# Two LSTMs inside a decoder: the inputs' share of the gates and the attention's values, in pieces of 128 columns, one in each step

## The chip, the cores and the metric

The kernel runs on one core of one Trainium2 chip. The metric is the device time of one execution in microseconds. Three runs of the kernel before gave 2397.09, 2397.65 and 2398.21 us; the median is 2397.65.

## What is computed

A decoder of four blocks, each with an attention, a cross attention and a feed-forward part, works on x of 8 sequences with 112 tokens and 256 features. The change lies in the first part alone, an attention whose queries and keys come from two LSTMs, and in which the two differ only by their weights:

```
xW = jnp.einsum('bsd,gd->sbg', x, Wih) + b
def step(carry, xt):
    h, c = carry
    gates = xt + h @ Whh.T
    i, f, g, o = jnp.split(gates, 4, axis=-1)
    c = jax.nn.sigmoid(f) * c + jax.nn.sigmoid(i) * jnp.tanh(g)
    h = jax.nn.sigmoid(o) * jnp.tanh(c)
    return ((h, c), h)
...
v = (hidden_states @ Wv.T + bv)
hq = _lstm(hidden_states, Wih_q, Whh_q, b_q)
hk = _lstm(hidden_states, Wih_k, Whh_k, b_k)
```

Small networks then turn hq and hk into queries and keys, and v is attended. Each LSTM has 112 steps that follow one on another: a step needs h of the step before it. The term xW needs no h, nor does v.

## The kernel before

All is in fp32. A step of one LSTM (line 645 on) is a chain over three engines. Eight matmuls on TensorE (line 649) multiply h with the 256 x 1024 recurrent weights. The batch is only 8, so h stands as weights of 128 x 32 and the gates' 1024 columns are moved past it in four quarters, each into its own 32 partitions of the PSUM tile g. ScalarE takes sigmoid and tanh of g (660, 661); VectorE makes the new cell in three operations (666, 668, 669); ScalarE its tanh (671); VectorE h (673) and its transpose hT (675), which is what the next step's matmuls wait for. GpSimd copies hT into hs, where the attention will find it (676). The two LSTMs, l = 0 and 1, take turns in each step t, so one's TensorE work lies beside the other's chain.

The inputs' share enters through TensorE as well. xw holds xW with its bias for 16 steps at a time (128 rows: 8 sequences x 16 steps). Four matmuls with a picking matrix as weights (`from_inputs`, line 627) start the tile g of step t + 1 with the right rows of xw, just after the recurrent matmuls of step t. xw itself is made by `inputs(m, l, half)` (line 617): two matmuls of 128 x 128 weights by 512 columns through the helper at line 410, then one addition of the bias on VectorE (622). The first four pieces, for steps 0 to 15, stand ahead of the loop; the other 24 are put at every fourth step (t = 2, 6, 10 and so on, lines 677 and 678). The PSUM tiles "mm" of these pieces have two buffers, and so has g.

After the loop, `l0_attn` makes the values: for each of the 8 sequences two matmuls of 112-column weights by 256 columns (line 569) and a bias addition (571). Then `l0_attend` begins with `unit` (line 705), whose matmuls take hs of the first LSTM, then of the second, and goes on to queries, keys, scores and the rest.

The order of each engine's instructions is settled when the program is built: a scheduler places them by priorities and estimated times, except inside a `tc.manual_schedule` block, where the engines named keep the order in which the code is written. Before the change the LSTMs are not in such a block. Weights lie in a ring of eight buffers, loaded through SyncE's queue when `w.done` frees buffers; the values' weights and bias are in the ring from the start.

In the trace each fp32 matmul instruction stands as two MATMULs, called passes below: a piece of 512 columns is four passes, line 649 is 16 per step and LSTM, line 627 is 8.

Of the kernel before, what the change touches and what calls it, by code (L numbers as in the profile page):

```python
# [24 lines left out]
AF = mybir.ActivationFunctionType  # L25
ALU = mybir.AluOpType
AX = mybir.AxisListType
ET = mybir.EngineType
PSUM = bass.MemoryType.PSUM

P = 128
S, NB, D = 112, 8, 256
# [323 lines left out]
class _Kernel:  # L356
# [198 lines left out]
    def l0_attn(self):  # L555
        nc, tc, w = self.nc, self.tc, self.w
        with ExitStack() as outer:
            keep = outer.enter_context(tc.tile_pool(name="l0a", bufs=1))
            hs = self.t(keep, [P, 2, 2, NB, S], "hs")
            vv = self.t(keep, [P, NB, 4, 64], "vv")  # L560
            with tc.tile_pool(name="ps_l0a", bufs=2, space=PSUM) as ps, tc.tile_pool(name="l0a_x", bufs=1) as px:
                xs = self.t(px, [P, 2, S // 16, NB, 16], "xs")
                self.ln_T_mm(ps, xs)
                self.lstm(hs, xs, ps)
                w.done("l0a_b_k")
                wv = w("l0a_wv", 2)
                bv = w("l0a_bv").rearrange("p (h d) -> p h d", h=4)
                for b in range(NB):
                    pm = self.t(ps, [P, 512], "mm")[:S, :D]
                    self.mm(pm, [(x, wv[:, k, :]) for k, x in enumerate(self.tokens(b))])  # L570
                    nc.vector.tensor_tensor(
                        vv[:S, b], pm.rearrange("p (h d) -> p h d", h=4), bv[:S], ALU.add
                    )
            self.l0_attend(hs, vv)
        w.done("l0a_bv")

# [16 lines left out]
                )  # L593
                self.nc.scalar.copy(self.xnT[:, kc, half * HT : (half + 1) * HT], tp[:, :HT])

    def lstm(self, hs, xs, ps0):

        nc, tc = self.nc, self.tc
        G = range(4)
        whh = [self.w("l0a_hh_q", 2), self.w("l0a_hh_k", 2)]
        wih = [self.w("l0a_ih_q", 2), self.w("l0a_ih_k", 2)]
        bias = [self.w("l0a_b_q"), self.w("l0a_b_k")]
        pick = self.c("pick").rearrange("p (r m) -> p r m", r=16)
        with tc.tile_pool(name="ps_lstm", bufs=2, space=PSUM) as ps, tc.tile_pool(  # L610
            name="lstm", bufs=2
        ) as work, tc.tile_pool(name="lstm_c", bufs=1) as cpool:

            xw = self.t(cpool, [P, 2, S // 16, 1024], "xw")
            cell = [self.t(cpool, [P, 64], f"cell{l}") for l in range(2)]

            def inputs(m, l, half):
                cols = slice(512 * half, 512 * half + 512)
                pm = self.t(ps0, [P, 512], "mm")
                steps = [xs[:, k, m, :, :].rearrange("p b r -> p (b r)") for k in range(2)]  # L620
                self.mm(pm, [(x, wih[l][:, k, cols]) for k, x in enumerate(steps)])
                nc.vector.tensor_tensor(xw[:, l, m, cols], pm, bias[l][:, cols], ALU.add)

            def from_inputs(t, l):
                g = self.t(ps, [P, 256], f"g{l}")
                for j in G:
                    nc.tensor.matmul(  # L627
                        g[32 * j : 32 * j + 32, :],
                        pick[:, t % 16, :],
                        xw[:, l, t // 16, 256 * j : 256 * j + 256],  # L630
                        start=True,
                        stop=t == 0,
                        skip_group_check=True,
                    )
                return g

            for l in range(2):
                for half in range(2):
                    inputs(0, l, half)
            later = [(m, l, half) for m in range(1, S // 16) for l in range(2) for half in range(2)]  # L640
            gs = [from_inputs(0, l) for l in range(2)]
            hT = [None, None]
            for t in range(S):
                for l in range(2):
                    g = gs[l]
                    if t > 0:
                        for c in range(2):
                            for j in G:
                                nc.tensor.matmul(  # L649
                                    g[32 * j : 32 * j + 32, :],  # L650
                                    hT[l][:, c, :],
                                    whh[l][:, c, 256 * j : 256 * j + 256],
                                    start=False,
                                    stop=c == 1,
                                    skip_group_check=True,
                                )
                    if t + 1 < S:
                        gs[l] = from_inputs(t + 1, l)
                    sg = self.t(work, [P, 256], f"sg{l}")
                    nc.scalar.activation(sg[:, :192], g[:, :192], AF.Sigmoid)  # L660
                    nc.scalar.activation(sg[:, 192:], g[:, 192:], AF.Tanh)
                    ig, fg, og, gg = (sg[:, 64 * i : 64 * i + 64] for i in range(4))
                    if t == 0:
                        nc.vector.tensor_tensor(cell[l], ig, gg, ALU.mult)
                    else:
                        nc.vector.tensor_tensor(cell[l], cell[l], fg, ALU.mult)
                        tmp = self.t(work, [P, 64], f"tmp{l}")
                        nc.vector.tensor_tensor(tmp, ig, gg, ALU.mult)
                        nc.vector.tensor_tensor(cell[l], cell[l], tmp, ALU.add)  # L669
                    th = self.t(work, [P, 64], f"th{l}")  # L670
                    nc.scalar.activation(th, cell[l], AF.Tanh)  # L671
                    h = self.t(work, [P, 64], f"h{l}")
                    nc.vector.tensor_tensor(h, og, th, ALU.mult)  # L673
                    hT[l] = self.t(work, [P, 2, 32], f"hT{l}")
                    nc.vector.transpose(hT[l].rearrange("p c b -> p (c b)"), h)  # L675
                    nc.gpsimd.tensor_copy(hs[:, l, :, :, t], hT[l][:, :, :NB])
                if t % 4 == 2 and later:
                    inputs(*later.pop(0))

    def l0_attend(self, hs, vv):  # L680

# [1563 lines left out]
```

## Time and profile before

| what | us |
|---|---|
| median of three runs | 2397.65 |
| profiled execution | 2397.02 |
| its span, first to last instruction | 2395.2 |
| first recurrent matmul (step 1) starts | 34.88 |
| recurrent matmuls of the last step start (first, second LSTM) | 428.50, 430.24 |
| values' matmuls | 429.50 to 437.8 |
| first matmul of the attention's first unit | 437.82 |

From 36 to 376 us, where the late pieces are, TensorE is counted busy 318 us, VectorE 204, ScalarE 131, GpSimd 43; the granted TensorE clock is 1.00. The bias additions are 28 of 0.692 us at line 622 and 8 of 0.424 us at line 571. The waits of that stretch are led, GpSimd's aside, by ScalarE's tanh for the cell (122.2 us over 183 times), weight loads of line 649 for hT (101.8 us), ScalarE's sigmoid for the recurrent matmuls (78.3 us) and h for the tanh (69.9 us).

How to read it: times are microseconds from the span's start. PE is TensorE's matmuls and PEld its weight loads, DVE is VectorE, ACT ScalarE, POOL GpSimd. `out<-in` are tiles by the program's names. A matmul's row gives its weights' shape (128*32) and its moving operand's (128x256); the start is recorded, the end is modelled, so that rows which follow one another overlap. A timeline merges equal instructions that follow each other into one row with a count; brackets give idle time of the engine before it and what ended that.

### The profile page before, as it was taken

Reading aid. Unit: us, or ns where it says so; the run is one execution under the profiler, and the core shown is the slowest. Engines: PE = TensorE matmul, PEld = TensorE weight load, DVE = VectorE, ACT = ScalarE, POOL = GpSimd, SP = SyncE. Lnnn points to the kernel's source line nnn. Section 1 sums busy time; section 2 is a strip of 40 time slices with the busy share of each in tenths; the row PEclk is TensorE's granted clock in tenths of the full one; section 3 lists DMA queues with packets and bytes.
Section 4 is the critical chain, followed back from the end, with each engine's and each line's share of the span. In section 5 each row is a group of like instructions: output and inputs, shape, how many; then the busy total and the mean of one; then the engine's idle time right before and its main releaser. Section 6 shows DMA issues by size and latency. Waiting matters only on the chain.

```text
span 2395.2 us, 43373 instructions
## 1 busy us (share of the span) xinstructions
PE 2135.7 (89%) x17096; PEld 1269.8 (53%) x17096; DVE 1427.7 (60%) x3994; ACT 774.4 (32%) x2157; POOL 216.3 (9%) x415
## 2 busy tenths in 40 slices
PE   6999999999898899899998869899999999899944
PEld 3444444466566566546664436466555556556622
DVE  4655566586455577543987557767740223667687
ACT  2333334462111355420111111466311110346522
POOL 0111111000011100000222331100000000200000
PEclk9999999899999999899999979999999999899956
DMA  4000000000100000001001011000111100000000
GB/s 188 2 2 2 2 20 35 30 19 18 53 1 15 19 2 19 18 27 53 1 19 36 19 44 38 16 2 19 53 36 63 42 0 1 1 1 2 2 0 16
DMA packets 10732, 55.95 MB, mean 23 GB/s; under 512 B 1834, under 2 KB 3626, under 8 KB 5793
## 3 DMA queue, kind: packets, MB, share of 16 engines
q1 hardware_dynamic: 8304, 44.57, 5.2%
q0 software_dynamic: 2080, 7.07, 0.9%
q8 instruction: 136, 2.23, 0.4%
q10 hardware_dynamic: 144, 1.54, 0.2%
q14 instruction: 68, 0.55, 0.1%
HBM read 52.23 MB, written 0.92 MB: 22 GB/s over the span
## 4 chain that ended last, share of the span: by engine, by line
PE 68%; DVE 20%; issue 5%; ACT 4%; DMA 2%; POOL 1%; DVEq 0%; ACTq 0%; POOLq 0%
PE mm L410 30%; PE gu L410 6%; PE tr L1197 6%; PE g L649 6%; PE sc L410 4%; PE av L1213 3%; PE tr L410 2%; DVE rot L1506 1%; ACT sg L660 1%; PE mm L799 1%; PE av L410 1%; ACT th L671 1%; DVE hT L675 1%; PE s L410 1%; DVE h L673 1%
## 5 line engine op out<-in xcount | busy, mean ns | idle before, releaser
L649 PE MATMUL g<-w,hT 128*32 128x256 f32 x3552 | 237.3, 384 | 26.2 <-DVE hT L675 25.9
L1197 PEld LDWEIGHTS tr<-cst,xe 112*125 112x125 f32 x1152 | 151.6, 188 | 94.7 <-issue 38.3
L1184 DVE TENSOR_REDUCE xnm<-sc 112x1 f32<-112x375 f32 x384 | 184.7, 541 | 28.6 <-PE sc L410 28.0
L410 PE MATMUL mm<-xnT,w 128*128 128x448 f32 x432 | 182.6, 560 | 18.8 <-DVE qT L1509 5.3
L1197 PE MATMUL tr<-cst,xe 112*125 112x112 f32 x1152 | 192.9, 289 | 7.1 <-DVE xeT L1205 4.3
L410 PE MATMUL mm<-hT,w 128*128 128x448 f32 x512 | 193.0, 539 | 0.0
L649 PEld LDWEIGHTS g<-w,hT 128*32 128x32 f32 x3552 | 95.4, 109 | 168.2 <-DVE hT L675 125.0
L410 PEld LDWEIGHTS mm<-hT,w 128*128 128x128 f32 x512 | 97.1, 190 | 94.4 <-issue 94.4
L627 PE MATMUL g<-xw,cst 128*32 128x256 f32 x1792 | 138.0, 379 | 0.0
L1205 DVE COPY xeT<-tr 125x336 f32<-125x336 f32 x192 | 97.3, 507 | 67.3 <-PE tr L1197 60.4
L1203 ACT COPY xeT<-tr 125x336 f32<-125x336 f32 x192 | 85.3, 444 | 159.4 <-PE tr L1197 159.4
L410 PEld LDWEIGHTS mm<-xnT,w 128*128 128x128 f32 x432 | 78.0, 193 | 104.2 <-issue 54.2
L410 PE MATMUL mm<-w,hT 128*112 128x256 f32 x576 | 131.8, 389 | 0.0
L1188 ACT ACTIVATE xe<-sc,xnm 112x375 f32<-112x375 f32 x256 | 126.6, 582 | 11.2 <-DVE xnm L1184 11.2
L410 PE MATMUL gu<-xnT,w 128*128 128x448 f32 x320 | 127.6, 554 | 1.6 <-DVE hT L1351 1.2
L410 PEld LDWEIGHTS mm<-w,hT 128*112 128x112 f32 x576 | 103.8, 182 | 26.8 <-issue 3.9
L660 ACT ACTIVATE sg<-g 128x192 f32<-128x192 f32 x224 | 74.1, 331 | 104.4 <-PE g L649 92.5
L671 ACT ACTIVATE th<-cell 128x64 f32<-128x64 f32 x224 | 57.4, 256 | 147.7 <-DVE cell L669 147.4
L673 DVE TENSOR_TENSOR h<-sg,th 128x64 f32<-128x64 f32 x224 | 50.5, 225 | 85.5 <-ACT th L671 85.5
L2099 DVE COPY wq<-tr 128x256 bf16<-128x256 bf16 (+1 forms) x12 | 4.6, 421 | 161.6 <-PE tr L2098 161.6
L410 PE MATMUL mm<-w,oT 128*112 128x256 f32 x288 | 75.8, 413 | 22.1 <-DVE oT L1686 13.8
L410 PEld LDWEIGHTS gu<-xnT,w 128*128 128x128 f32 x320 | 60.3, 193 | 61.5 <-issue 54.9
(404 smaller groups left out, 3667.9 us busy)
## 6 DMA issues: line engine op xcount, KB each, us to landing
w<-in_w SPq DMA_DIRECT2D x33, 1024.0 KB, 4.9
raw<-in_wq POOLq DMA_DIRECT2D x3, 1024.0 KB, 5.2
w<-in_w SPq DMA_DIRECT2D x3, 896.0 KB, 6.9
wi<-in_wint POOLq DMA_DIRECT2D x3, 768.0 KB, 6.2
w<-in_w SPq DMA_DIRECT2D x2, 768.0 KB, 4.4
ctxT<-in_ctxT ACTq DMA_DIRECT2D x1, 1500.0 KB, 8.3
cx<-in_ctx POOLq DMA_DIRECT2D x1, 1500.0 KB, 20.9
w<-in_w SPq DMA_DIRECT2D x2, 512.0 KB, 3.5
```

What stands on the lines that cost most here:

```text
L410: self.nc.tensor.matmul(out, lhsT, rhs, start=i == 0, stop=i == len(pairs) - 1)
L627: nc.tensor.matmul(g[32 * j : 32 * j + 32, :], pick[:, t % 16, :], xw[:, l, t // 16, 256 * j : 256 * j + 256], start=True, stop=t == 0, sk ...
L649: nc.tensor.matmul(g[32 * j : 32 * j + 32, :], hT[l][:, c, :], whh[l][:, c, 256 * j : 256 * j + 256], start=False, stop=c == 1, skip_group ...
L660: nc.scalar.activation(sg[:, :192], g[:, :192], AF.Sigmoid)
L671: nc.scalar.activation(th, cell[l], AF.Tanh)
L673: nc.vector.tensor_tensor(h, og, th, ALU.mult)
L1184: nc.vector.tensor_reduce(nm, sc, AX.X, ALU.max, negate=True)
L1188: nc.scalar.activation(e, sc, AF.Exp, bias=nm)
L1197: nc.tensor.transpose(tp[:CH, i * S : (i + 1) * S], e[:, i * CH : (i + 1) * CH], self.ident[:S, :S])
L1203: nc.scalar.copy(eT, src)
L1205: nc.vector.tensor_copy(eT, src)
L1213: nc.tensor.matmul(avs[b][32 * j : 32 * j + 32, c * S : (c + 1) * S], values[b % 2][:CH, i, 4 * c + j, :], eTs[b, c, j][:, i, :], start=i ...
```

## The change

`inputs` now takes a first column and a width. Ahead of the loop it still makes the four pieces of 512 columns; all else is cut into pieces of 128 columns: 6 x 2 x 8 = 96 of the inputs' share and, by a new function `values`, 8 x 2 = 16 of the values. They form one list of 112 in the order of need. One is made ahead of the loop and one in each step 0 to 110. Its matmuls are written after the second LSTM's matmuls and the picking matmuls for its next step; its bias addition is returned as a function and written on VectorE between the second LSTM's cell and its h. The loop is wrapped in a manual schedule of TensorE, VectorE and ScalarE. The loop over the values behind the LSTMs is gone, and the call that frees the LSTMs' weights stands behind both.

```
-                self.lstm(hs, xs, ps)
-                w.done("l0a_b_k")
-                wv = w("l0a_wv", 2)
...
-                for b in range(NB):
-                    pm = self.t(ps, [P, 512], "mm")[:S, :D]
-                    self.mm(pm, [(x, wv[:, k, :]) for k, x in enumerate(self.tokens(b))])
...
+                self.lstm(hs, xs, vv, ps)
+            w.done("l0a_b_k")
...
-            def inputs(m, l, half):
-                cols = slice(512 * half, 512 * half + 512)
-                pm = self.t(ps0, [P, 512], "mm")
+            def inputs(m, l, a, n):
+                cols = slice(a, a + n)
+                pm = self.t(ps0, [P, 512], "mm")[:, :n]
                 steps = [xs[:, k, m, :, :].rearrange("p b r -> p (b r)") for k in range(2)]
                 self.mm(pm, [(x, wih[l][:, k, cols]) for k, x in enumerate(steps)])
-                nc.vector.tensor_tensor(xw[:, l, m, cols], pm, bias[l][:, cols], ALU.add)
+                def biased():
+                    nc.vector.tensor_tensor(xw[:, l, m, cols], pm, bias[l][:, cols], ALU.add)
+                return biased
+            def values(b, half):
+                cols = slice(half * P, half * P + P)
+                pm = self.t(ps0, [P, 512], "mm")[:S, :P]
+                self.mm(pm, [(x, wv[:, k, cols]) for k, x in enumerate(self.tokens(b))])
+                out = vv[:S, b].rearrange("p h d -> p (h d)")[:, cols]
+                def biased():
+                    nc.vector.tensor_tensor(out, pm, bv[:S, cols], ALU.add)
+                return biased
...
-            later = [(m, l, half) for m in range(1, S // 16) for l in range(2) for half in range(2)]
+            pieces = [(inputs, m, l, P * i, P) for m in range(1, S // 16) for l in range(2) for i in range(8)]
+            pieces += [(values, b, half) for b in range(NB) for half in range(2)]
+            inputs(*pieces.pop(0)[1:])()
...
+            with tc.manual_schedule(engines={ET.PE, ET.DVE, ET.Activation}):
+                for t in range(S):
+                    for l in range(2):
...
+                        if t + 1 < S:
+                            gs[l] = from_inputs(t + 1, l)
+                        if l == 1 and pieces:
+                            make, *which = pieces.pop(0)
+                            biased = make(*which)
...
+                            nc.vector.tensor_tensor(cell[l], cell[l], tmp, ALU.add)
+                        if l == 1 and biased:
+                            biased = biased()
+                        th = self.t(work, [P, 64], f"th{l}")
...
-                if t % 4 == 2 and later:
-                    inputs(*later.pop(0))
```

More of the change, by code (lines that the diff above doesn't have):

```diff
@@ L563, in l0_attn @@
                 self.ln_T_mm(ps, xs)
-                self.lstm(hs, xs, ps)
-                w.done("l0a_b_k")
-                wv = w("l0a_wv", 2)
-                bv = w("l0a_bv").rearrange("p (h d) -> p h d", h=4)
-                for b in range(NB):
-                    pm = self.t(ps, [P, 512], "mm")[:S, :D]
-                    self.mm(pm, [(x, wv[:, k, :]) for k, x in enumerate(self.tokens(b))])
-                    nc.vector.tensor_tensor(
-                        vv[:S, b], pm.rearrange("p (h d) -> p h d", h=4), bv[:S], ALU.add
-                    )
+                self.lstm(hs, xs, vv, ps)
+            w.done("l0a_b_k")
             self.l0_attend(hs, vv)
@@ L594, in ln_T_mm, with lstm @@
                 self.nc.scalar.copy(self.xnT[:, kc, half * HT : (half + 1) * HT], tp[:, :HT])
-    def lstm(self, hs, xs, ps0):
-        nc, tc = self.nc, self.tc
+    def lstm(self, hs, xs, vv, ps0):
+        nc, tc, w = self.nc, self.tc, self.w
         G = range(4)
@@ L638, in lstm @@
                 for half in range(2):
-                    inputs(0, l, half)
-            later = [(m, l, half) for m in range(1, S // 16) for l in range(2) for half in range(2)]
+                    inputs(0, l, 512 * half, 512)()
+            pieces = [(inputs, m, l, P * i, P) for m in range(1, S // 16) for l in range(2) for i in range(8)]
+            pieces += [(values, b, half) for b in range(NB) for half in range(2)]
+            inputs(*pieces.pop(0)[1:])()
             gs = [from_inputs(0, l) for l in range(2)]
@@ L642, in lstm @@
             hT = [None, None]
[L643 to L676, printed above, removed]
-                if t % 4 == 2 and later:
-                    inputs(*later.pop(0))
@@ new lines, in lstm @@
+            wv, bv = w("l0a_wv", 2), w("l0a_bv")
+            with tc.manual_schedule(engines={ET.PE, ET.DVE, ET.Activation}):
+                for t in range(S):
+                    for l in range(2):
+                        g = gs[l]
+                        if t > 0:
+                            for c in range(2):
+                                for j in G:
+                                    nc.tensor.matmul(
+                                        g[32 * j : 32 * j + 32, :],
+                                        hT[l][:, c, :],
+                                        whh[l][:, c, 256 * j : 256 * j + 256],
+                                        start=False,
+                                        stop=c == 1,
+                                        skip_group_check=True,
+                                    )
+                        if t + 1 < S:
[3 more added lines that the diff above has]
+                            biased = make(*which)
+                        sg = self.t(work, [P, 256], f"sg{l}")
+                        nc.scalar.activation(sg[:, :192], g[:, :192], AF.Sigmoid)
+                        nc.scalar.activation(sg[:, 192:], g[:, 192:], AF.Tanh)
+                        ig, fg, og, gg = (sg[:, 64 * i : 64 * i + 64] for i in range(4))
+                        if t == 0:
+                            nc.vector.tensor_tensor(cell[l], ig, gg, ALU.mult)
+                        else:
+                            nc.vector.tensor_tensor(cell[l], cell[l], fg, ALU.mult)
+                            tmp = self.t(work, [P, 64], f"tmp{l}")
+                            nc.vector.tensor_tensor(tmp, ig, gg, ALU.mult)
+                            nc.vector.tensor_tensor(cell[l], cell[l], tmp, ALU.add)
+                        if l == 1 and biased:
+                            biased = biased()
+                        th = self.t(work, [P, 64], f"th{l}")
+                        nc.scalar.activation(th, cell[l], AF.Tanh)
+                        h = self.t(work, [P, 64], f"h{l}")
+                        nc.vector.tensor_tensor(h, og, th, ALU.mult)
+                        hT[l] = self.t(work, [P, 2, 32], f"hT{l}")
+                        nc.vector.transpose(hT[l].rearrange("p c b -> p (c b)"), h)
+                        nc.gpsimd.tensor_copy(hs[:, l, :, :, t], hT[l][:, :, :NB])
```

## The prediction

> **What bounds the kernel now.** The page's chain says only that TensorE carries 68% of the end and line 649 6% of it; the change touches the first 440 us, so I read that stretch by its own views. First the windows: from 36 to 376 us PE is busy 318 of 340 us, the granted clock 1.00. That looks full, but the ends of matmuls are modelled, so I count from start to start. TensorE alone, around a step that makes one piece of the inputs' share, in order of time (start us, duration us):
>
> ```profile
> 39.22 1.07 PE L649 MATMUL g<-w,hT 128*32 128x256 f32 x16
> 40.10 0.61 PE L627 MATMUL g<-xw,cst 128*32 128x256 f32 x8
> 40.65 1.98 PE L410 MATMUL mm<-w,xs 128*128 128x512 f32 x4
> 42.56 1.07 PE L649 MATMUL g<-w,hT 128*32 128x256 f32 x16
> 43.45 0.61 PE L627 MATMUL g<-xw,cst 128*32 128x256 f32 x8
> 43.88 1.05 PE L649 MATMUL g<-w,hT 128*32 128x256 f32 x16
> 44.74 0.61 PE L627 MATMUL g<-xw,cst 128*32 128x256 f32 x8
> 45.76 0.42 PE L649 MATMUL g<-w,hT 128*32 128x256 f32 x4 [0.40 <-DVE hT L675]
> ```
>
> Call line 649 A (A0 and A1 for the two LSTMs), line 627 B, and the piece P. Start to start, A holds TensorE 0.88 (0.86 when it follows B unhindered, 43.88 to 44.74), B 0.43 (43.45 to 43.88), 0.55 when a piece follows (40.10 to 40.65), and the 512-column piece 1.91 (40.65 to 42.56). From A1 to the next A1: 0.88+0.55+1.91+0.89+0.43 = 4.66, which is what lies between 39.22 and 43.88. In such a step TensorE is the bound and nothing waits for hT.
>
> Now a step without a piece, late in the loop; TensorE alone, then from the view of all engines what leads from A0 to the next A0:
>
> ```profile
> 427.01 1.07 PE L649 MATMUL g<-w,hT 128*32 128x256 f32 x16 [0.23 <-DVE hT L675]
> 427.90 0.61 PE L627 MATMUL g<-xw,cst 128*32 128x256 f32 x8
> 428.50 1.07 PE L649 MATMUL g<-w,hT 128*32 128x256 f32 x16
> ...
> 431.24 6.75 PE L410 MATMUL mm<-w,xnT 128*112 128x256 f32 x30
> 437.82 2.42 PE L410 MATMUL tr<-hs,w 128*128 128x448 f32 x6
> ```
>
> ```profile
> 428.21 0.33 ACT L660 ACTIVATE sg<-g 128x192 f32<-128x192 f32 x1 [0.40 <-PE g L649]
> ...
> 428.97 0.23 DVE L669 TENSOR_TENSOR cell<-cell,tmp 128x64 f32<-128x64 f32 x1
> 429.29 0.26 ACT L671 ACTIVATE th<-cell 128x64 f32<-128x64 f32 x1 [0.64 <-DVE cell L669]
> ...
> 429.58 0.23 DVE L673 TENSOR_TENSOR h<-sg,th 128x64 f32<-128x64 f32 x1 [0.38 <-ACT th L671]
> ...
> 429.94 0.24 DVE L675 STREAM_TRANSPOSE hT<-h 128x64 f32<-128x64 f32 x1
> ...
> 430.24 0.59 PEld L649 LDWEIGHTS g<-w,hT 128*32 128x32 f32 x16 [0.47 <-DVE hT L675]
> ```
>
> Here the recurrence is the bound: A0 at 427.01, the next at 430.24, 3.22 us, all of it latency. TensorE's own work is 2 x (0.88+0.43) = 2.62, so about 0.6 us of each step is free. The four steps of a cycle with a piece take 4.67+3.33+3.25+3.23 = 14.48 us against 4 x 3.22 = 12.9: each of the 24 late pieces adds 1.6 us, though TensorE has 2.4 us of slack in its four steps. From A0 of step 1 (34.88) to A0 of step 111 (428.50) it is 393.6 us: 110 x 3.22 = 354.6, pieces 38, about 1 for a few steps that run 0.3 long.
>
> **The change, part by part.** (1) Removed: 24 x 1.6 = 38 us that the pieces add. (2) Added: in each of 111 steps, P of four passes of 128 columns (a matmul in fp32 stands as two in the trace), after B1 in TensorE's order; the order listing of the built kernel shows just that: A0 B0 A1 B1 P. Nearest row for a pass of 128 columns:
>
> ```profile
> L410 PE MATMUL av<-vb,eT x128: 272/273/421, 1169.0 to 1273.3; 112*112 112x128 f32 x128
> ```
>
> Sixteen of these stand as one row of 2.00 us at 1169.00: (2.00-0.27)/15 = 0.115 apart, each with its own weights. The 512-column piece was 1.91 with passes 0.43 apart, so 4 x 0.43 plus 0.19 that the weight loads at its two ends expose; another 0.12 lies between B and P (0.55 less 0.43). I give the small piece the same ends: 0.12 + 0.19 + 4 x 0.11 = 0.75 us. TensorE's step is then 0.88+0.43+0.86+0.43+0.75 = 3.36 us (from three decimals: 0.886, 0.432, 0.863, 0.432, 0.746). That is over 3.22: every step becomes bound by TensorE, by 0.14.
>
> Here a rule of the Trainium skill speaks against the change: "TensorE: Matmul & The Clock Gate", Part 3, The mechanism, says that a weight load overlaps matmuls in flight only when their row groups differ. All loads of P use all rows, so by the rule each pass would pay its load, which by the row of the 512-column piece's first passes is 0.10 more (0.53 against 0.43 apart): P 0.75+3x0.10 = 1.06 (unrounded), the step 3.67, and 110 steps cost 110 x 0.31 = 34 us more. The av row has the same kind of loads and 0.115 between passes, so I go by the row; the rule is the case "slower" below.
>
> (3) VectorE: 24 x 0.69 us at line 622 leave, 96 pieces' and 16 values' bias additions come. Rows give 0.692 for 512 columns and 0.424 for 256, so about 0.29 for 128. It stands before h of the second LSTM, so it makes a wait: if P is late, h, its transpose and A1 stand behind it. With A1 0.88+0.43 = 1.31 behind A0 (as in the timeline at 202.89 and 204.21), cell(1) at line 669 starts 3.41 after A0, th(1) 3.73, h(1) 4.02. P's last pass starts 1.31+0.86+0.55+0.43 = 3.15 after A0 and is out 0.27 later, at 3.43. The addition runs from about 3.65 to 3.94, beside th on ScalarE, and ends 0.08 before h starts. So I cost it at nothing; the cover is thin. That spacing gave A1 to A1 3.33 (204.21 to 207.54), still under 3.36. If the cover were gone whole, the step would be 3.33+0.29 = 3.62. ScalarE keeps its order.
>
> (4) The values leave the end. Now 30 of their passes run from 431.24, and the first unit of the attention starts at 437.82, 9.32 after A0 of step 111. It needs only hs of the first LSTM, which POOL has copied about 3.45 after A0 (the transpose ends at 3.17, the copy takes 0.23); with the handover it starts at 3.5. Gain 5.8. Sixteen values' pieces sit in steps 95 to 110 and are in the sum as P. The second LSTM's hs (some 1.3 later) comes as the first unit's four passes of 0.375 end.
>
> (5) One 128-column piece stands ahead of step 0: 4 x 0.11, +0.44. SP's queue and POOL keep their orders by the listing; the two weight loads at 429.63 go with the end of the loop, and their readers are stages away. Behind the loop all engines' orders are the same, so what the loop gains goes to the end.
>
> Sum: A0 of step 111 at 34.88+0.44+110x3.36+1 = 405.9 in place of 428.5: 22.6. With 5.8 it is 28.4. The profiled execution was 2397.02 (span 2395.2); 2368.6 for it. The median of the runs is 0.6 above: 2369.
>
> **The rivals.** *Forecast, 2369 (chance 0.65):* TensorE bound at 3.36, sizes as above; 0.05 us either way in the step is 5.5 us, 2363 to 2375.
>
> *The bias addition holds h up (0.16):* P is handed over later than I read, or the addition is over 0.37 long. For it: 0.08 of cover, and it is in order ahead of h. Against it: VectorE's idle time before h in the rows above is 0.38, all of it waiting for th. Half exposed the step is 3.48: 2382. Exposed whole, 3.62 gives 2397, no change.
>
> *The ends cost nothing (0.10):* the first load of P may be drawn under B, and A's under P. Then TensorE needs 3.05 to 3.2 and the recurrence bounds at 3.22 to 3.33: about 2358 in the middle, 2353 at the end. Against it: every one of the exposed ends recurs in each of the 24 pieces.
>
> *Slower (0.09):* weight loads bound each pass, as the rule above says. 3.67 gives 2403. It decides from 0.09 us more per pass, where the step reaches 3.62 and the gain is gone. Some 112-column transposes do stand 0.15 to 0.19 apart, which speaks for it; they are firsts of a group.
>
> That the change does not spread the work is excluded by the listing; that the clock sinks under the denser work is not, but it is 1.00 over the whole loop at 94% busy.
>
> **How the numbers follow.** 2369. The range takes the forecast with its bounds, the lower middle of the case of free ends and the half exposed addition with 4 us above: 2357 to 2386; outside lie the whole exposure, the slower case and the very low end, under 0.2. A measurement of this kernel tells about 0.2% (4.8 us) from no change. Faster: 0.65+0.10+0.12 of the addition's 0.16 = 0.87; within 0.2% 0.04; slower 0.09.
>
> **What would show it.** Right: A0 to A0 3.3 to 3.4 in every step from 1 to 110, no step of 4.67; P about 0.63 from its start to A0; A0 waiting for nothing on VectorE; the bias addition about 0.29 and h still waiting for th; the first unit about 3.5 after the last A0. Wrong: passes of P 0.2 apart (weight loads), h released by the addition, or A0 waiting for hT with steps near 3.22 (free ends).

## The result and the profile after

The changed kernel took 2366.95 us in the median of four runs (2358.11 to 2372.21), the kernel before 2397.37 (2395.19 to 2398.21): a ratio of 0.9871, 95% interval 0.9834 to 0.9908. Forecast were 2369 and a range of 2357 to 2386. The profiled execution was 2358.11, its span 2356.3.

Line 649 has become line 663, 627 is 637, 675 is 694. TensorE alone in the middle of the loop, from A1 on, with the weight load of this A1 put in from the view of all engines:

```profile
204.58 0.60 PEld L663 LDWEIGHTS g<-w,hT 128*32 128x32 f32 x16 [0.26 <-DVE hT L694]
204.62 1.05 PE L663 MATMUL g<-w,hT 128*32 128x256 f32 x16
205.48 0.61 PE L637 MATMUL g<-xw,cst 128*32 128x256 f32 x8
206.02 0.71 PE L410 MATMUL mm<-w,xs 128*128 128x128 f32 x4
206.67 1.07 PE L663 MATMUL g<-w,hT 128*32 128x256 f32 x16
207.55 0.61 PE L637 MATMUL g<-xw,cst 128*32 128x256 f32 x8
207.99 0.39 PE L663 MATMUL g<-w,hT 128*32 128x256 f32 x3
```

From 204.62 to 207.99 is one step, 3.37. No matmul row has an idle time in brackets, and 0.86+0.54+0.65+0.88+0.44 adds up to the step. The piece holds TensorE 0.65 until A0, after 0.54 from B1 on. One weight load does wait: that of A1 sits idle 0.26 for the second LSTM's hT (25.7 us over 95 times from 46 to 376 us). It costs nothing, since A1's matmuls still start 0.43 to 0.44 after B0, as in the kernel before where nothing holds them up. But hT is finished at 204.52, 0.10 before A1 starts, so the second LSTM's chain is nearly as long as TensorE's work.

The bias addition and what stands around it, from all engines' view of the step before:

```profile
203.34 0.23 DVE L686 TENSOR_TENSOR cell<-cell,tmp 128x64 f32<-128x64 f32 x1
203.49 0.28 DVE L619 TENSOR_TENSOR xw<-mm,w 128x128 f32<-128x128 f32 x1
203.66 0.26 ACT L690 ACTIVATE th<-cell 128x64 f32<-128x64 f32 x1 [0.80 <-DVE cell L686]
203.95 0.23 DVE L692 TENSOR_TENSOR h<-sg,th 128x64 f32<-128x64 f32 x1 [0.18 <-ACT th L690]
```

The addition runs beside the tanh and ends at 203.77; h still waits 0.18 for the tanh. Behind the loop, the second LSTM's last recurrent matmuls (A1 of step 111) and the first unit of the attention:

```profile
407.10 1.07 PE L663 MATMUL g<-w,hT 128*32 128x256 f32 x16 [0.23 <-DVE hT L694]
...
409.30 3.27 PE L410 MATMUL tr<-hs,w 128*128 128x448 f32 x8 [1.13 <-POOL hs L695]
```

A0 of step 111 started at 405.80; the attention's first unit starts 3.50 later, and waits for POOL's copy of hs, no more for the values.

### The profile page after: what moved, and what is told of

It reads as the page before. It is cut to its first block, busy times and chain, and to the rows that moved or that the text cites. A ratio compares the mean times of both kernels' runs of the same rounds, so it can differ in the third digit from the quotient of the medians.

```text
span 2356.3 us, 44094 instructions
## 1 busy us (share of the span) xinstructions
PE 2120.1 (90%) x17416; PEld 1299.3 (55%) x17416; DVE 1430.1 (61%) x4074; ACT 771.3 (33%) x2157; POOL 217.0 (9%) x415
## 4 chain that ended last, share of the span: by engine, by line
PE 75%; DVE 16%; issue 4%; ACT 2%; DMA 2%; POOL 1%; POOLq 0%; DVEq 0%; ACTq 0%
PE mm L410 32%; PE g L663 9%; PE gu L410 6%; PE tr L1214 6%; PE sc L410 4%; PE g L637 4%; PE av L1230 3%; PE tr L410 1%; DVE rot L1523 1%; PE mm L816 1%; PE av L410 1%; PE s L410 1%; DMA cx<-in_ctx 1%; DVE nm L987 1%; DVE xnm L1201 1%
## 5 line engine op out<-in xcount | busy, mean ns | idle before, releaser
L410 PE MATMUL sc<-xkT,qT 32*112 32x375 f32 x768 | 89.8, 519 | 0.0
```

The source lines that it names most:

```text
L410: self.nc.tensor.matmul(out, lhsT, rhs, start=i == 0, stop=i == len(pairs) - 1)
```

## Two clocks of the comparison: the loop and what lies behind it

Every kernel here runs the same instructions in the same order from kT's first addition (line 726 before, 743 after) to the end. I take its start as the mark for what the change does, and the rest apart. "Half" is the time in that rest at a granted clock of 0.5, summed over the clock records of the trace; between the first hT and kT it is 0 in every run. Each row is one traced execution, and its time is that of this execution.

| kernel | traced execution | first hT of step 0 | last hT of the first LSTM (step 111) | kT | rest | half |
|---|---|---|---|---|---|---|
| before | 2397.02 | 34.59 | 431.43 | 442.77 | 1952.5 | 244.4 |
| after | 2358.11 | 33.89 | 408.69 | 414.35 | 1942.0 | 220.7 |
| e0_again | 2360.56 | 35.06 | 409.87 | 415.53 | 1943.3 | 227.5 |
| a_third | 2371.59 | 34.85 | 409.62 | 415.29 | 1954.5 | 242.9 |
| b_again | 2397.25 | 34.74 | 431.48 | 442.82 | 1952.7 | 244.3 |
| b_third | 2397.78 | 34.81 | 431.51 | 442.85 | 1953.1 | 244.3 |
| e1_manual_512 | 2387.62 | 34.77 | 431.47 | 442.80 | 1943.0 | 227.3 |
| e2_no_manual | 2365.87 | 34.49 | 409.38 | 414.99 | 1949.1 | 237.7 |
| e3_values_after | 2373.14 | 34.95 | 407.56 | 418.91 | 1952.4 | 240.9 |
| e4_256 | 2392.72 | 35.50 | 432.22 | 437.89 | 1953.1 | 246.1 |
| e5_tiled | 2335.19 | 35.11 | 390.90 | 396.57 | 1936.8 | 209.1 |
| e6_add_twice | 2368.95 | 34.42 | 412.25 | 418.11 | 1949.1 | 234.0 |
| e7_no_pieces | 2346.25 | 34.67 | 393.03 | 404.37 | 1940.1 | 213.7 |

kT moved from 442.77 to 414.35: 28.4 us, the sum of the forecast. The other 10.5 of the profiled execution lie in the rest. That the sum is met to 0.1 us is partly chance: e0_again and a_third, the same kernel, give 27.2 and 27.5.

## The experiments

**e0_again, b_again, b_third, a_third: what lies behind the loop.** The two kernels unaltered.

> The changed kernel once more, unaltered. Theory: the LSTMs and the values give 28.4 us in every execution (the first addition of kT, line 743, starts at 414.35 again, within 0.1), and the further 10.7 us of the profiled execution are no work of the change: they lie in later stages and go with where half-clock stretches of TensorE fell. Then the total moves between executions by some 10 us while the loop doesn't, and the ratio's middle lies near 0.988 (2397 less 28.4). Rival: the later stages gain 10 us for good, from the earlier start; then nearly all executions lie near 2358.

> The kernel before, profiled once more, for what lies behind the LSTMs. Theory: from kT's first addition to the end all kernels here run the same instructions, and that stretch takes 1937 to 1953 us by where the half-clock stretches fall, about 0.43 us per us at half clock; kT's first addition starts at 442.8 within 1 us, and the rest fits that line again (1942 at 222 us of half clock, 1952 at 243). Rival: the rest belongs to the kernel; then it is 1952.5 again whatever the clock did.

> The kernel before once more, as the last look met the same half-clock time as the first and so told nothing apart. Theory: kT's first addition at 442.8; the rest by the line 1843.4 + 0.446 us per us at half clock, whatever the kernel. Rival: 1952.5 belongs to this kernel.

> The changed kernel once more. Theory: kT's first addition at 414.3 to 415.6 (the first hT lies between 33.9 and 35.1), the rest by the same line. Rival: 1942 to 1943 belongs to this kernel.

e0_again: 2360.56 in the median (2356.35 to 2362.02, 5 runs), ratio 0.9859, 0.9836 to 0.9882. kT comes at 415.53, 1.2 later than in the first trace; 1.17 of it is there at the first hT already, which the theory had not allowed for. The traces place it in the first four pieces of 512 columns, ahead of the loop: these start at 22.67 us in the first trace and at 22.57 here, so the load and the normalisation are not the cause. Their passes begin 0.85 apart and later stand 0.43 apart, as in the loop. The change to 0.43 comes with the trace's first record of a clock of 1.00, at 26.18 us in the first trace and at 28.63 here.

The kernel before moved more than its first runs showed: 17 runs of that comparison lie between 2384.84 and 2400.59, 0.7% apart, where the prediction had counted on telling 0.2%. Their mean granted clock goes with it, from 0.954 in the three near 2385 to 0.948 in the slowest.

By its nearness to 2358, e0_again alone favoured the rival. b_again and b_third told nothing apart: both met 244.3 us of half clock again and 1952.7 and 1953.1 of rest. a_third did: the changed kernel with kT at 415.29 as ever and a rest of 1954.5 in place of 1942.0, with 22 us more at half clock. And e1 (below) has the loop of the kernel before to 0.1 us and a rest of 1943.0. So the rest follows the half-clock time, about 0.45 us per us, and isn't owned by a kernel; the line in the expectation of b_third gives 1951.7 for a_third, 2.8 short. Set side by side instruction by instruction on VectorE, a_third falls 12.6 us behind the first trace of the same kernel, and about 10.7 of these come up in half-clock stretches that one of the two has and the other has not; between e1 and the kernel before it is about 6.4 of 9.4. What sets where those stretches fall was not tried and stays open.

**e1_manual_512: the written-out order alone.** The changed kernel with the pieces as before:

```
-pieces = [(inputs, m, l, P * i, P) ... for i in range(8)]   # and the values
+pieces = [(inputs, m, l, 512 * i, 512) ... for i in range(2)]
-if l == 1 and pieces:
+if l == 1 and t % 4 == 2 and pieces:
```

with the bias addition behind hT of the second LSTM and the values behind the loop.

> Written-out order alone: pieces of 512 columns at every fourth step and the values behind the loop, as before the change, in the changed kernel's manual schedule (bias addition behind the second LSTM's hT). Theory: the order is the one that the scheduler chose anyway, so four steps take 14.5 us again, A0 of step 111 starts near 428 and the total stays near 2397. Rival: the order written out is itself a gain; then four steps fall to under 14 us and A0 of step 111 to under 415.

kT at 442.80 against 442.77, and steps of 4.81, 3.22, 3.22, 3.22 from hT to hT of the first LSTM, as before. The order written out is worth nothing in the loop. The total is 9.4 less, all of it in the rest; the total alone would have looked like a gain.

**e2_no_manual: the rest of the change without it.** `with tc.manual_schedule(...)` became `if True`.

> The changed kernel without its manual schedule: small pieces in each step, values in the loop, the scheduler's own order. Theory: the order that comes out is the same from step 1 on, so the step stays 3.37 and A0 of step 111 is at 405.8 within 0.3. Rival: the schedule matters; then the two differ by several us.

The step is 3.37, and from the first to the last hT of the first LSTM it is 374.9 against 374.8. What remains is the cut into pieces and the values' place.

**e3_values_after: the values back behind the loop.**

```
-pieces += [(values, b, half) for b in range(NB) for half in range(2)]
+for b in range(NB): ...   # behind lstm(), as before
```

> The changed kernel with the values behind the loop again. Theory: steps 95 to 110 fall from 3.36 to 3.22 (2 us), while the first unit of the attention starts 9.3 in place of 3.5 us after A0 of step 111 (5.8 us): kT's first addition comes 3.8 us after 414.35, near 418. Rival: the values' place is worth nothing; then 412 to 414.

Steps 95 to 110, which had the values' pieces, took 3.22, and kT came at 418.91: 4.6 later, 3.5 when the later first hT (34.95 against 33.89) is taken off.

**e7_no_pieces: the floor of the recurrence.** `pieces = []`, and `xw[:, l, t // 16, ...]` became `xw[:, l, 0, ...]`: it leaves out the inputs' share of steps 16 to 111.

> Leaves out the inputs' share of steps 16 to 111 (every step takes that of its place in the first 16) and has no piece in the loop; the values are made behind the loop as before. Theory: the floor of the recurrence, 3.22 in every step: A0 of step 111 near 34.4 + 110 x 3.22 + 1 = 390. So the pieces cost 16 us in all in the changed kernel. Rival: something other than the pieces keeps the step at 3.3 or more (the order written out); then it stays there.

3.22 in nearly every step; the last hT at 393.03, 15.7 ahead of the changed kernel's. From the first hT to the last it is 358.4 us against 374.8. So the pieces still cost 16 us there: TensorE's 0.14 to 0.15 over the recurrence, step by step.

**e4_256: half as many pieces of twice the width.** 256 columns at `t % 2 == 0`, values by whole sequences.

> Pieces of 256 columns, one in every second step (values: one sequence each). The ends are paid half as often: a piece is 0.31 + 4 x 0.216 = 1.18, TensorE needs 2 x 2.61 + 1.18 = 6.40 us in two steps, under 2 x 3.22 = 6.45. Theory: slack can't be saved up, since the recurrence waits for its own last step: 3.79 for the step with a piece, 3.22 to 3.33 for the one without, 3.5 to 3.56 in the mean, A0 of step 111 15 to 20 us later than 405.8 (421 to 426). Rival: the mean of TensorE's work counts; then 3.22 to 3.25 in the mean and A0 of step 111 near 391.

2382.55 in the median of ten (2379.13 to 2392.77), slower than the changed kernel (0.9965 of the kernel before, 0.9947 to 0.9984): steps of 3.92 and 3.22 from hT to hT, 3.57 in the mean. A0 of step 111 starts at 429.30, past the 421 to 426 expected. TensorE alone (A0, B0, A1, B1, P, A0):

```profile
203.67 1.07 PE L663 MATMUL g<-w,hT 128*32 128x256 f32 x16 [0.40 <-DVE hT L694]
204.56 0.61 PE L637 MATMUL g<-xw,cst 128*32 128x256 f32 x8
205.13 1.07 PE L663 MATMUL g<-w,hT 128*32 128x256 f32 x16
206.01 0.61 PE L637 MATMUL g<-xw,cst 128*32 128x256 f32 x8
206.56 1.13 PE L410 MATMUL mm<-w,xs 128*128 128x256 f32 x4
207.62 1.07 PE L663 MATMUL g<-w,hT 128*32 128x256 f32 x16
```

The work sums to under two floors, yet the loop is no faster than with 512 columns: A0 and A1 wait for their hT (A1 starts 1.46 after A0, where 1.32 is their work), and the piece then comes on top. Slack of one step can't be kept for the next. The step with a piece is 0.13 longer than I expected, about as much as that wait for A1. kT is 4.9 us earlier than before the change, by the values' place.

**e6_add_twice: how thin is the addition's cover.**

```
 if l == 1 and biased:
+    biased()
     biased = biased()
```

> Each bias addition in the loop written twice (the same result twice). Theory: one addition is hidden beside the tanh with 0.18 us left before h starts in the changed kernel's trace; a second adds about 0.2 to 0.28 on VectorE, so h starts 0.02 to 0.1 later and the second LSTM's round goes from 3.33 to 3.35 to 3.43: the step stays between 3.37 and 3.43, A0 of step 111 0 to 7 us later. Rival: the addition already lies on the path and costs its whole length; then the step goes to 3.65 and A0 of step 111 to 436.

The step is mostly 3.37 and 3.41 in turn, 3.40 in the mean: as expected. A second addition of 0.28 adds 0.03 to the step, so the first is free, and most of a second.

**e5_tiled: the same pieces without their ends.**

```
+def tiled(pm, pairs, n):
+    for i, (x, y) in enumerate(pairs):
+        for a in range(0, n, 32):
+            z = min(a + 32, n)
+            nc.tensor.matmul(pm[a:z, :], x[:, a:z], y, start=i == 0, stop=i == 1, skip_group_check=True)
```

> The same pieces, but each with its 128 (112) weight columns in four column tiles of 32, as the recurrent matmuls have them. Theory: what a piece costs beyond its passes is 0.31 us of weight loads at its two ends, and tiles of 32 columns load beside running tiles, so a piece costs 4 x 0.11 = 0.44 in place of 0.75; TensorE's step falls to 3.05, and the recurrence bounds at 3.22 to 3.33: A0 of step 111 comes 4 to 15 us before 405.8. Rival: the number of instructions per piece (16 passes in place of 4) or switching from B to a piece costs as such; then the step stays at 3.36 or grows.

2337.60 in the median (2332.83 to 2352.17), 0.9782 of the kernel before, 0.9752 to 0.9812, against 0.9859 for the changed kernel in the same comparison. It is faster than both; 19.0 of the 23.0 us between the two medians stand in the loop's traces, from the first hT to the last. TensorE, with the weight load of the last A1:

```profile
203.44 1.07 PE L675 MATMUL g<-w,hT 128*32 128x256 f32 x16
204.32 0.61 PE L649 MATMUL g<-xw,cst 128*32 128x256 f32 x8
204.75 0.62 PE L616 MATMUL mm<-w,xs 128*32 128x128 f32 x16
205.19 1.05 PE L675 MATMUL g<-w,hT 128*32 128x256 f32 x16
206.06 0.61 PE L649 MATMUL g<-xw,cst 128*32 128x256 f32 x8
206.63 0.37 PEld L675 LDWEIGHTS g<-w,hT 128*32 128x32 f32 x12 [0.44 <-DVE hT L706]
206.63 0.64 PE L675 MATMUL g<-w,hT 128*32 128x256 f32 x8
```

B to piece is 0.43 in place of 0.54, piece to A0 0.44 in place of 0.65, with four times as many matmuls. The recurrence is the bound again: A1 starts 0.57 after B0, when its weights have waited 0.44 for hT, and the step is 3.195. The last hT came 17.8 us ahead of the changed kernel's profiled execution (19.0 ahead of e0_again's), a little more than the 4 to 15 I gave, since 3.195 is below what I took for the floor. The rows put the 0.03 between the starts of h and hT (0.33 here and in the changed kernel, 0.36 in e7 and in the kernel before where a step has no piece); why they lie closer stays open.

## Why the prediction was right

- *TensorE bound at 3.36:* 3.37 from A0 to A0 in 87 of 110 steps, 3.35 or 3.36 in 15 with values' pieces; 8 odd steps took 3.44 to 3.61, 1.0 us over in all, the 1 us that was allowed. The forecast took the ends from the 512-column piece; they were 0.11 before the first pass, and 0.20 for the gap behind it and the one at A0 together. The pieces' loads and passes are

```profile
L410 PEld LDWEIGHTS mm<-w,xs x372: 186/190/192, 40.5 to 351.7; 128*128 128x128 f32 x186
L410 PE MATMUL mm<-w,xs x372: 275/275/377, 40.5 to 351.8; 128*128 128x128 f32 x186
L619 DVE TENSOR_TENSOR xw<-mm,w x93: 281/283/293, 41.3 to 352.2; 128x128 f32<-128x128 f32 x93
```

Four loads of 0.19 in a piece of 0.65 do overlap passes; the four passes start 0.213, 0.112 and 0.112 apart. The rule, as the prediction took it, by which each pass would pay its load (step 3.67), fails here, as the row of the other stage had said. What is paid belongs to the two borders where a piece on the whole array meets tiles of 32 columns: inside the piece the same loads cost nothing, and in e5, where all have one shape, the borders cost nothing. e5 shortens each load as well (0.11 in place of 0.19), so it does not tell whether the loads' length has a part in it. The loop between first and last hT fell by 22.0 us (396.8 to 374.8); the forecast's terms 3.36 and 1 us of odd steps gave 23.0, and 110 x 0.007 accounts for most of the difference.
- *The bias addition at nothing:* right, with 0.18 of cover in place of 0.08. It took 0.283 (0.29 estimated) and started 3.56 after A0, not 3.65: its row begins before the cell's addition ends. The rival's wait does exist, but it took a second addition (e6) to bring it out, at 0.03 a step.
- *The values, 5.8:* from the last hT of the first LSTM to kT it was 11.3 and is 5.7: 5.7.
- *The piece ahead of the loop, 0.44:* right, though hidden in the totals, since the start of the loop moves by up to 1.6 from run to run (33.89 to 35.50). Until the first record of a clock of 1.00 the passes ahead of the loop take twice as long, so half of that time is lost. With it taken off, the first hT comes 9.46 to 9.47 us after the first pass of these pieces in the changed kernel's traces and 9.02 us after it in e1 and e7, which have no piece there: 0.44. The kernel before takes 9.34. That the profiled execution began 0.7 early, by the clock ahead of the loop (e0_again), makes up by luck for most of the 1.0 that the loop gave less.
- *The end:* "what the loop gains goes to the end" held for the marks, not for one execution. The 10.5 us beyond it in the profiled execution go with the half-clock stretches of later stages; the prediction had asked for the clock only inside the loop, where it was 1.00. The median of 2367 lies 2 us under the forecast, and the same luck is the likely cause, not shown: of its four executions only one was traced, but the granted clock is 0.953 and 0.952 in the two of 2358 and 2362, 0.949 and 0.947 in the two of 2372. The rival of free ends, named as the faster case, fails in the changed kernel and is what e5 makes of it.
- *A label:* the rows at 427.01 and 430.24 us, which the prediction calls A0, are A1 of steps 110 and 111; A0 of step 111 is the row at 428.50. The step of 3.22 is the same for both.

The kernel gained because a wait of 1.6 us per large piece, which the recurrence could not take back, became 0.14 per step; 16 us of the former 38 are still paid.

## What to carry to other kernels

Beside a recurrence that has some free time in every step, filler work is worth cutting until one cut fits into one step's slack; a piece that overruns delays the chain for good, and the slack of steps without a piece is lost. Count an engine's slack from start to start, and add what going over to the filler and back costs; giving the filler the tile shape of its neighbours took away 0.31 of 0.75 us. Judge a local change by a mark just behind it: the same instructions after it took from 1937 to 1955 us.

## What was not expected

The half-clock time behind the loop went from 209 to 246 us between executions and went with 18 us in the rest, about three quarters of a per cent of the whole, for kernels with the same instructions there. And in e5 the 128-column passes in four tiles of 32 started almost together, 0.007 us apart, and the next four 0.110 after the first: as fast as one pass on the whole array (0.112), with no time to be seen for their weights.
